# Fill tokens, x blocks and routing counts of a mixture-of-experts block with linear attention, on one Trainium2 core

## The chip, the core and the metric

The kernel runs on one core of a Trainium2 chip. A core has five engines that run their own instruction streams: TensorE (PE, matrix products, with a weight load PEld ahead of each), VectorE (DVE), ScalarE (ACT), GpSimd (POOL) and SyncE (SP, which here only issues transfers). They wait for one another by semaphores. Sixteen DMA engines move data between the chip's memory and the core's on-chip memories. The time is the device time of one execution in microseconds; lower is better.

## The reference

Input x is (8, 1024, 256) in float32: 8 sequences of 1024 tokens. It is normalised per token to xn = (x - mean) / sqrt(var + 1e-5). The output is x + attention(xn) + experts(xn).

```python
# attention: 16 heads of 16; no softmax, causal by a running sum
q = elu(xn @ Wq.T) + 1;  k = elu(xn @ Wk.T) + 1;  v = xn @ Wv.T
out   = einsum('blhd,blhde->blhe', q, cumsum(k (x) v, axis=tokens))
denom = clip(einsum('blhd,blhd->blh', q, cumsum(k, axis=tokens)), 1e-6)
attention = (out / denom) @ Wo.T

# experts: 8 of 256 -> 512 -> 256, the two with the largest logits per token
logits = xn @ Wr + br
weights, experts = top_k(logits, 2);  weights = softmax(weights)
experts(xn) = sum over the 2: weight * ((silu(xn @ W1[e]) * (xn @ W3[e])) @ W2[e])
```

## The kernel before

**Blocks and tiles.** The 8192 tokens are 16 blocks of 512 (`NBLK`), each of 4 chunks of 128. Attention runs over blocks, in 11 steps each (`block_steps`, 176 steps). The experts run over tiles of 128 tokens that go to one expert: 8192 tokens with 2 experts each make 128 full tiles, and up to 7 more because each expert's list ends in a part-filled tile, 135 in all (`NF`), of which 132 (`NM`) are always run. The first 25 tiles (`N1`) hold tokens of blocks 0 to 3 only, and so can start before the other blocks are read. The other tiles are listed once all blocks are routed.

**Start.** An order written by hand (`manual_schedule`) normalises blocks 0 to 3, turns them (features onto partitions), computes their logits, routes them (`route(0, FB)`), and lists the first 25 tiles (`first_batch`).

**The main loop**, `for j in range(NM + 1)`, then runs one expert tile per turn (`ffn_step`): it requests the tile after next's W1 and W3 (512 KB each) on SP's queue and gathers x rows and table entries on GpSimd's queue three tiles ahead; `ffn_hidden` makes gate and up products (32 matmuls, `gu_ps`), `ffn_turn` turns the next tile, and `ffn_out` multiplies the previous tile's hidden values by W2 (8 matmul passes, `y_ps`) and scales by the routing weight. `ffn_store` adds the tile's rows to the output by a GpSimd scatter with accumulation. Between the tiles attention goes on: `attend_upto(n)` runs attention up to step n. Its last phase, from `READ` = tile 22 on, spreads the rest by a quotient of the tile's number.

**Blocks 4 to 15** are handled in turns j = 0 to 11: `moments(t, 2)` computes mean and variance for two blocks at once on VectorE (`bn_stats`, then a Newton iteration for 1/sqrt in small operations), `normalise(t)` writes xn on ScalarE from the block's x into a tile of its own (two buffers), `turn(t)` transposes it on TensorE into `xnT`, which is stored to memory for attention, and `logits_of(t)` follows. `load_x(t + 3)` requests the x block three further on ScalarE's queue; x has three buffers. After every fourth block `route` takes the four: the two largest logits (a dozen VectorE operations on 128x128), counts per expert by three matmul passes into `cnt_ps`, places within an expert's list (`slot`), and the routing weights (`tab`). `route` is a generator: each `yield` is a point at which the caller can go on with other work. In the main loop it is run to its end at once.

**Fill tokens.** A part-filled tile has rows without a token. Each such row still scatters (a zero contribution), to some row of the output. Two rows of one tile must not add to the same output row, so each row p of an expert's short tile needs a token that this expert has not got. `other_tokens` finds 128 of these for each expert among the first 256 tokens: it ranks the tokens that the expert lacks (`others`, `rank_ps`), builds 16 one-hot matrices on VectorE (`at`) and multiplies each by a column of token numbers (`num_ps`). It runs at tile 8 (`LISTS - 4`). `second_batch`, from tile 12 (`LISTS`) to 21, lists the other tiles by one-hot products (`held_ps`) in parts, one part per turn, and places the fill tokens in the list's empty entries (`fill`, `fills`).

**Order.** Outside the hand-written start, a planner orders each engine's instructions by its own estimates of durations and by the order in the program; `in_order` keeps an instruction at its place. Buffers come from pools (`f_x`, `f_two`, `ps_y`) whose rotation adds waits.

Of the kernel before, what the change touches and what calls it, by code (L numbers as in the profile page):

```python
# [46 lines left out]
F32 = mybir.dt.float32  # L47
I32 = mybir.dt.int32
AF = mybir.ActivationFunctionType
ALU = mybir.AluOpType  # L50
AX = mybir.AxisListType

P = 128
# [9 lines left out]
def tile_attention_moe(  # L63
# [14 lines left out]
    nc = tc.nc  # L78
# [37 lines left out]
    f_one = ctx.enter_context(tc.tile_pool(name="f_one", bufs=1))  # L116
    f_two = ctx.enter_context(tc.tile_pool(name="f_two", bufs=2))
    f_three = ctx.enter_context(tc.tile_pool(name="f_three", bufs=3))
    f_x = ctx.enter_context(tc.tile_pool(name="f_x", bufs=3))

    early = ctx.enter_context(ExitStack())
    e_one = early.enter_context(tc.tile_pool(name="e_one", bufs=1))
# [20 lines left out]
    def load_x(t, queue):  # L143
        xbs[t] = f_x.tile([P, NCH, H], F32, tag="xb", name=f"xb{t}")
        in_order(queue.dma_start(out=xbs[t], in_=xf[t]))
# [45 lines left out]
    def iota(name, n, step, base, mult):  # L191
# [19 lines left out]
        number1, pattern=[[1, 2 * FT]], base=1, channel_multiplier=2 * FT,  # L211
        allow_small_or_imprecise_dtypes=True,
    )
    token = const.tile([P, 2], F32, name="token")
    nc.gpsimd.iota(
        token, pattern=[[P, 2]], base=1, channel_multiplier=1,
        allow_small_or_imprecise_dtypes=True,
    )
    count = f_one.tile([P, E, 1], F32, name="count")
    nc.gpsimd.iota(  # L220
        count[:, :, 0], pattern=[[N, E]], base=0, channel_multiplier=0,
# [70 lines left out]
    def normalise(t):  # L292
        xb = xbs.pop(t)
        less, rstd = (tab[:, t * NCH : (t + 1) * NCH, w] for w in (1, 2))
        xn = f_two.tile([P, NCH, H], F32, tag="xn", name="xn")
        for c in range(NCH):
            if t < FB and (c % 2 == 0 or t == FB - 1):
                nc.vector.tensor_scalar(
                    xn[:, c, :], xb[:, c, :], rstd[:, c : c + 1], less[:, c : c + 1],
                    ALU.mult, ALU.add,  # L300
                )
            else:
                nc.scalar.activation(
                    xn[:, c, :], xb[:, c, :], AF.Identity, bias=less[:, c : c + 1],
                    scale=rstd[:, c : c + 1],
                )
        scaled[t] = xn

    def turn(t):
        xn = scaled.pop(t)  # L310
# [53 lines left out]
    nc.gpsimd.memset(new, 1.0)  # L364
    nc.gpsimd.memset(new[:, :, 0:1], 0.0)
    slot = f_one.tile([P, 2, NT], F32, name="slot")
    others = f_one.tile([P, 2, E], F32, name="others")

    def route(a, b):

# [35 lines left out]
        both = f_two.tile([P, E, n], F32, tag="both", name="both")  # L406
        by_tile = both.rearrange("p e t -> p t e")
        nc.vector.tensor_tensor(by_tile, hits[:, 0], hits[:, 1], ALU.add)

        reset = new[:, :, 0:n]  # L410
        if n < MOST:
# [6 lines left out]
        )  # L418
        cnt_ps = ps_y.tile([P, E * n + E], F32, tag="y", name="cnt_ps")
        for m, what in ((upto_neg, both), (ones, run)):  # L420
            nc.tensor.matmul(
                cnt_ps[:, 0 : E * n], lhsT=m, rhs=what.rearrange("p e t -> p (e t)"),
                start=(m is upto_neg), stop=(m is ones),
            )
        nc.tensor.matmul(
            cnt_ps[:, E * n :], lhsT=ones, rhs=run[:, :, n - 1], start=True, stop=True
        )
        if a == 0:
            nc.vector.tensor_scalar(others, by_tile[:, 0:2, :], -1.0, 1.0, ALU.mult, ALU.add)
        yield  # L430
        pos = f_one.tile([P, E, n], F32, tag="pos", name="pos")
        nc.vector.tensor_tensor(
# [17 lines left out]
        nc.vector.tensor_copy(tab[:, tiles, 0], wt)  # L450
        nc.vector.tensor_tensor(tab[:, second, 0], diff, wt, ALU.mult)
        nc.vector.tensor_copy(tab[:, second, 1:3], tab[:, tiles, 1:3])
        for t in range(a, b):
            del turned[t]
        yield

    def other_tokens():


        rank_ps = ps_y.tile([P, 2, E], F32, tag="y", name="rank_ps")  # L460
        nc.tensor.matmul(
            rank_ps.rearrange("p t e -> p (t e)"), lhsT=before,
            rhs=others.rearrange("p t e -> p (t e)"), start=True, stop=False,
            skip_group_check=True,
        )
        nc.tensor.matmul(
            rank_ps[:, 1, :], lhsT=ones, rhs=others[:, 0, :], start=False, stop=True,
            skip_group_check=True,
        )
        rank = f_one.tile([P, 2, E], F32, name="rank")  # L470
        nc.vector.tensor_copy(rank, rank_ps)
        other = f_one.tile([P, E], F32, name="other")
        num_ps = ps_y.tile([P, E], F32, tag="y", name="num_ps")
        for e in range(E):
            for T in range(2):
                at = f_two.tile([P, P], F32, tag="lgT", name="at")
                nc.vector.tensor_scalar(
                    at, cols[:, 0:P], rank[:, T, e : e + 1], others[:, T, e : e + 1],
                    ALU.is_equal, ALU.mult,
                )  # L480
                nc.tensor.matmul(
                    num_ps[:, e : e + 1], lhsT=at, rhs=token[:, T : T + 1],
                    start=(T == 0), stop=(T == 1),
                )
        nc.vector.tensor_copy(other, num_ps)
        return other

    def sizes(up):

# [103 lines left out]
    def first_batch():  # L593
# [32 lines left out]
        batches[0] = tab_d[0], te_i, num_i, src_i, acc_d, src_i  # L626
        firsts.append(taken)
        yield
    def second_batch(taken, other):

        rows = sizes(True)
        left = f_one.tile([P, E], F32, name="left")
# [13 lines left out]

        short = f_one.tile([P, E], F32, name="short")
        nc.vector.tensor_scalar(short, rows, 1.5, None, ALU.is_lt)
        fill = f_one.tile([P, E], F32, name="fill")
        nc.vector.tensor_scalar(fill, other, -1.0, row[:, 0:1], ALU.add, ALU.subtract)  # L650
        nc.vector.tensor_tensor(fill, fill, short, ALU.mult)
        nc.vector.tensor_scalar(fill, fill, row[:, 0:1], None, ALU.add)
        fills = f_one.tile([P, N2], F32, name="fills")
        for e in range(E):
            mine = fills if e == 0 else f_two.tile([P, N2], F32, tag="mine", name="mine")
            nc.vector.tensor_scalar(
                mine, te, float(e), fill[:, e : e + 1], ALU.is_equal, ALU.mult
            )
            if e > 0:
                nc.vector.tensor_tensor(fills, fills, mine, ALU.add)  # L660
        num_i = const.tile([P, N2], I32, name="of2_i")
        all_held = f_one.tile([P, N2], F32, name="all_held")
        yield
        for j in range(2):
            for a in range(0, NT, 16):
                ps = ps_y.tile([P, N2], F32, tag="y", name="held_ps")
                for b in range(a, a + 16, PART):
                    at, held = one_hot(in_row, place, of_tiles, number, j, b, N2)
                    for i in range(PART):
                        nc.tensor.matmul(  # L670
                            ps, lhsT=at[:, i, :], rhs=held[:, i, :],
                            start=(b + i == a), stop=(b + i == a + 15),
                        )
                if j == 0 and a == 0:
                    nc.vector.tensor_copy(all_held, ps)
                else:
                    nc.vector.tensor_tensor(all_held, ps, all_held, ALU.add)
                yield
        nc.vector.tensor_copy(num_i, all_held)
        _, src_i = tokens(all_held, N2, NT, "2_i")  # L680
# [256 lines left out]
    with tc.manual_schedule(engines={EN.DVE, EN.Activation, EN.PE, EN.Pool}):  # L937
# [21 lines left out]
            next(q)  # L959
        routing = route(0, FB)  # L960
        next(routing)
        for o in range(KC):
            next(qs[o])
        next(ks[0])
# [173 lines left out]
    for j in range(NM + 1):  # L1138
        if j + 1 < NM:
            ffn_norm(j + 1)  # L1140
        t = FB + j
        if t < NBLK:
            if j % 2 == 0:
                with tc.issue_after(last_token[0].ins):
                    for _ in moments(t, 2):
                        pass
            normalise(t)
            if t + 3 < NBLK:
                load_x(t + 3, nc.scalar)
            turn(t)  # L1150
            logits_of(t)
            if (j + 1) % ROUND == 0:
                for _ in route(t + 1 - ROUND, t + 1):
                    pass
        if j == LISTS - 4:
            with tc.issue_after(last_token[0].ins):
                other = other_tokens()
        if j == LISTS:
            in_order(
                nc.sync.dma_start(  # L1160
                    out=tab_d[1][1 : 1 + NS * P, :].rearrange("(p i) w -> p (i w)", p=P),
                    in_=tab.rearrange("p i w -> p (i w)"),
                )
            )
            in_order(nc.sync.dma_start(out=tab_d[1][0:1, :], in_=before[0:1, 0:3]))
            lists = second_batch(taken, other)
        if LISTS <= j < READ:
            next(lists)
        if LISTS <= j < LISTS + NBLK - FB:
            t = FB + j - LISTS  # L1170
            rows = slice(t * TB, (t + 1) * TB)
            in_order(nc.sync.dma_start(out=out_rows[rows, :], in_=x_rows[rows, :]))
        if j < LISTS:
            attend_upto(3 + j // 2)
        elif j < READ:
            attend_upto(AHEAD - 2 * (READ - j - 1))
        else:
            attend_upto(AHEAD + (NBLK * STEPS - AHEAD) * (j - READ + 1) // (NM - READ - 1))
        if j == N1 + 1:
            copied.append(j)  # L1180
            in_order(nc.sync.dma_start(out=out_rows[0 : FT * P, :], in_=acc_d[:, :]))
        ffn_step(j, LATE if N1 < j <= N1 + LATE else 0)
# [53 lines left out]
```

## Time and profile before

| | us |
|---|---|
| median of the runs | 1401.64 |
| lowest and highest of 3 | 1396.12, 1402.63 |
| profiled execution, its own time | 1416.01 |
| profiled execution, span of the trace | 1414.3 |
| TensorE busy within the span | 1347.8 |
| VectorE, ScalarE, GpSimd busy | 733.5, 492.4, 517.5 |
| mean granted TensorE clock | 0.979 of full |

The profile is of one execution, here one that took longer than the timed runs. A row of its tables names a line of the kernel, an engine, and the tiles written and read; "busy" is the sum over a row's instructions, and "idle before" is how long the engine stood before them and for whom. TensorE's ends are modelled, and its clock can be granted at half: then the same matmuls show as more busy time. Busy shares are averages over stages with different limits, so a stage table (busy time in each stretch of the span) is read beside them.

### The profile page before, as it was taken

How to read it: one execution, taken by the hardware profiler on the slowest of the kernel's cores; microseconds unless marked ns; L12 is line 12 of the kernel's file. 1: busy time of each engine (PE TensorE's matmuls, PEld its weight loads, DVE VectorE, ACT ScalarE, POOL GpSimd, SP SyncE). 2: the span in 40 equal slices, each digit the busy share in tenths (PEclk: the TensorE clock that was granted, in tenths of full speed). 3: DMA queues.
4: the chain of work that ended last, by engine and by line, in shares of the span. 5: the costliest groups of instructions: out<-in, count | busy, mean ns of one | idle time of the engine just before them, and what ended most of it. 6: DMA issues, size and time to landing. Idle time of an engine off the chain costs nothing.

```text
span 1414.3 us, 27960 instructions
## 1 busy us (share of the span) xinstructions
PE 1347.8 (95%) x10932; PEld 1145.2 (81%) x10932; DVE 733.5 (52%) x1448; ACT 492.4 (35%) x914; POOL 517.5 (37%) x448
## 2 busy tenths in 40 slices
PE   6798999999999999999999999999999999999995
PEld 4667778788888888888888888888888888878885
DVE  6695468867354453536363635435353635445451
ACT  4455333132251515251523324142413325151511
POOL 2323224222434434333433343353434443343422
PEclk9999799999999999999999999999999999999998
DMA  9677455345675656565655555575655656565652
GB/s 347 191 235 223 137 161 139 105 120 160 158 220 151 175 131 149 162 164 137 159 161 135 161 149 143 129 182 144 149 162 141 157 150 157 141 173 131 150 143 42
DMA packets 129412, 223.56 MB, mean 158 GB/s; under 512 B 14818, under 2 KB 53346, under 8 KB 128994
## 3 DMA queue, kind: packets, MB, share of 16 engines
q1 hardware_dynamic: 84306, 165.95, 37.3%
q0 software_dynamic: 38064, 43.22, 19.3%
q10 hardware_dynamic: 6912, 12.58, 2.5%
q8 instruction: 90, 1.47, 0.4%
q14 instruction: 40, 0.33, 0.1%
HBM read 187.91 MB, written 44.29 MB: 164 GB/s over the span
## 4 chain that ended last, share of the span: by engine, by line
PE 82%; DVE 11%; DMA 3%; ACT 3%; issue 1%; POOL 0%; POOLq 0%; DVEq 0%; ACTq 0%
PE gu_ps L1075 32%; PE y_ps L1092 14%; PE s_ps L823 5%; PE a_ps L886 4%; PE o_ps L864 4%; PE zq L726 4%; PE zkk L741 3%; PE zkv L741 3%; DMA xb<-in_x_dram 2%; PE kv_ps L838 2%; PE held_ps L670 2%; DVE rden L802 2%; PE xg_t L1045 2%; PE o_ps L857 2%; DVE ksum L791 2%; PE den L801 2%
## 5 line engine op out<-in xcount | busy, mean ns | idle before, releaser
L1075 PEld LDWEIGHTS gu_ps<-xgT,w 128*128 128x128 f32 x4224 | 499.6, 195 | 32.0 <-issue 18.7
L1075 PE MATMUL gu_ps<-xgT,w 128*128 128x128 f32 x4224 | 518.1, 280 | 4.2 <-DVE s_sb L830 3.8
L1024 POOL DMA_INDIRECT xg<-in_x_dram,src_i x132 | 129.7, 982 | 508.7 <-ACT xgT L1047 431.6
L1092 PE MATMUL y_ps<-w_sb,hT 128*128 x1056 | 258.5, 386 | 1.3 <-DVE hT L1084 0.7
L1101 POOL DMA_INDIRECT out_dram<-y,dst_i x107 | 174.8, 1634 | 187.2 <-DVE y L1097 87.4
L1084 DVE TENSOR_TENSOR hT<-gu_ps,hT 128x512 f32<-128x512 f32 x132 | 90.4, 685 | 243.1 <-PE gu_ps L1075 226.4
L1092 PEld LDWEIGHTS y_ps<-w_sb,hT 128*128 128x128 f32 x1056 | 192.3, 193 | 25.5 <-issue 3.9
L1081 ACT ACTIVATE hT<-gu_ps 128x512 f32<-128x512 f32 x132 | 78.8, 597 | 380.8 <-PE gu_ps L1075 375.5
L830 DVE TENSOR_TENSOR s_sb<-s_ps,causal 128x512 f32<-128x512 f32 x256 | 163.2, 683 | 74.3 <-PE s_ps L823 73.3
L1097 DVE TENSOR_SCALAR y<-y_ps,entry 128x256 f32<-128x256 f32 x132 | 63.6, 482 | 135.3 <-PE y_ps L1092 135.2
L1029 POOL DMA_INDIRECT entry<-tab_d,of_i x107 | 108.0, 1009 | 32.6 <-issue 31.4
L802 DVE RECIPROCAL rden<-den 128x512 f32<-128x512 f32 x32 | 105.4, 3329 | 3.3 <-PE den L801 3.2
L823 PE MATMUL s_ps<-qm,kT 32*128 32x256 f32 x1024 | 102.7, 409 | 2.9 <-DVE rden L802 1.5
L1047 ACT COPY xgT<-xg_t 128x256 f32<-128x256 f32 x132 | 49.1, 372 | 147.9 <-PE xg_t L1045 146.3
L891 ACT COPY at<-a_ps 128x256 f32<-128x256 f32 x64 | 23.8, 372 | 193.6 <-PE a_ps L886 193.6
L823 PEld LDWEIGHTS s_ps<-qm,kT 32*128 32x128 f32 x1024 | 58.4, 184 | 36.6 <-issue 19.5
L1036 ACT ACTIVATE xg<-xg,entry 128x256 f32<-128x256 f32 x132 | 79.5, 603 | 12.0 <-DVE st L267 11.8
L886 PE MATMUL a_ps<-wo_sb,oT 128*128 128x256 f32 x256 | 68.9, 392 | 4.4 <-DVE oT L872 4.2
L1101 POOL DMA_INDIRECT acc_d<-y,src_i x25 | 42.2, 1688 | 82.2 <-DVE y L1097 46.9
L864 PE MATMUL o_ps<-s_sb,va 128*32 128x128 f32 x2048 | 70.2, 276 | 0.0
L886 PEld LDWEIGHTS a_ps<-wo_sb,oT 128*128 128x128 f32 x256 | 47.9, 193 | 14.1 <-DVE oT L872 7.4
L864 PEld LDWEIGHTS o_ps<-s_sb,va 128*32 128x32 f32 x2048 | 52.2, 109 | 8.0
(187 smaller groups left out, 1480.6 us busy)
## 6 DMA issues: line engine op xcount, KB each, us to landing
w<-in_w_dram SPq DMA_DIRECT2D x264, 512.0 KB, 4.4
xnT_d<-xnT ACTq DMA_DIRECT2D x15, 512.0 KB
xnT<-xnT_d SPq DMA_DIRECT2D x15, 512.0 KB, 5.1
out_dram<-in_x_dram SPq DMA_DIRECT2D x12, 512.0 KB
out_dram<-at POOLq DMA_DIRECT2D x12, 512.0 KB
xb<-in_x_dram ACTq DMA_DIRECT2D x9, 512.0 KB, 6.9
w_sb<-in_w_dram SPq DMA_DIRECT2D x4, 1024.0 KB
xb<-in_x_dram SPq DMA_DIRECT2D x7, 512.0 KB, 14.6
```

The costliest lines, as they stand in the source:

```text
L741: nc.tensor.matmul(z[:, i, :], lhsT=xnTs[t][:, k, bass.ts(c + i, P)], rhs=wkv_sb[:, k, a, :], start=(k == 0), stop=(k == KC - 1),)
L802: nc.vector.reciprocal(rden[:, o, :], den)
L823: nc.tensor.matmul(s_ps[r][:, hh].rearrange("p a l -> p (a l)"), lhsT=kT[rows, hh, span], rhs=qm[rows, hh, :, span], start=True, stop=True,)
L830: nc.vector.tensor_tensor(sm, s_ps[r].rearrange("p k a l -> p (k a) l"), causal_b, ALU.mult)
L864: nc.tensor.matmul(o_ps[32 * r : 32 * r + 32, hh, :], lhsT=va[:, c, 4 * hh + r, a, :], rhs=s_sb[r][:, 2 * hh + a, :], start=(first and a = ...
L886: nc.tensor.matmul(a_ps, lhsT=oT[:, hh, :], rhs=wo_sb[:, hh, :], start=(hh == 0), stop=(hh == 1),)
L1024: nc.gpsimd.indirect_dma_start(out=xg[j], out_offset=None, in_=x_rows[:, :], in_offset=bass.IndirectOffsetOnAxis(ap=src_i[:, i : i + 1], a ...
L1029: nc.gpsimd.indirect_dma_start(out=entry[j], out_offset=None, in_=table[:, :], in_offset=bass.IndirectOffsetOnAxis(ap=num_i[:, i : i + 1], ...
L1075: nc.tensor.matmul(ps[:, i, :], lhsT=w13[:, k, bass.ts(i, P)], rhs=xgT[j][:, k, :], start=(k == 0), stop=(k == KC - 1),)
L1084: nc.vector.tensor_tensor(hT, gu[1], hT, ALU.mult)
L1092: nc.tensor.matmul(y_ps, lhsT=hT[:, i, :], rhs=w2_sb[:, bass.ds(e * (IC * H) + i * H, H)], start=(i == 0), stop=(i == IC - 1),)
L1101: nc.gpsimd.indirect_dma_start(out=rows[:, :], out_offset=bass.IndirectOffsetOnAxis(ap=dst_i[:, i : i + 1], axis=0), in_=ys.pop(j), in_off ...
```

## The change

Five things are changed.

1. *Fill tokens by partition.* Instead of 128 tokens by rank, each partition p looks for one tile number T such that token T*128 + p has not been given to the expert. In `route`, `without` is 0 for tokens that the expert has and 64 - T for the others; a maximum over the tiles, kept over the rounds in `free`, gives the lowest free T per partition and expert (0 where there is none). A partition without any takes the token of partition 0, which a matmul with `ones` spreads (`at_0_ps`). `other_tokens(short)` now runs within `second_batch`, in its second part; the 3 rank passes, the 16 one-hot matrices and the 16 products are gone.
2. *x is normalised in place*, in the tile that it was read into; the two `xn` buffers go, and x has five buffers.
3. *x is read five blocks ahead*: blocks 7 and 8 are requested at the first turn, and block t + 5 after `turn(t)`.
4. *Counts a tile later.* `route` has one more `yield`, after `both`; the main loop runs it up to there after a fourth block, and the rest (counts, places, weights, `without`) at the beginning of the next turn. The counts' matmuls of these rounds keep their place in the program's order.
5. *Attention's last phase* divides by `NM - READ - 4` instead of `NM - READ - 1`.

```diff
-    f_x = ctx.enter_context(tc.tile_pool(name="f_x", bufs=3))
+    f_x = ctx.enter_context(tc.tile_pool(name="f_x", bufs=5))
...
+    from_end = iota("from_end", NT, 1, -NT, 0)
...
     def normalise(t):
-        xn = f_two.tile([P, NCH, H], F32, tag="xn", name="xn")
...
-                    xn[:, c, :], xb[:, c, :], AF.Identity, bias=less[:, c : c + 1],
+                    xb[:, c, :], xb[:, c, :], AF.Identity, bias=less[:, c : c + 1],
                     scale=rstd[:, c : c + 1],
...
     def route(a, b):
...
         nc.vector.tensor_tensor(by_tile, hits[:, 0], hits[:, 1], ALU.add)
+        yield
...
-            nc.tensor.matmul(
+            counted = nc.tensor.matmul(
...
+            if a > 0:
+                in_order(counted)
...
-        if a == 0:
-            nc.vector.tensor_scalar(others, by_tile[:, 0:2, :], -1.0, 1.0, ALU.mult, ALU.add)
...
+        without = f_one.tile([P, E, n], F32, tag="pos", name="without")
+        nc.vector.scalar_tensor_tensor(
+            without, both, -1.0, from_end[:, tiles].unsqueeze(1).to_broadcast([P, E, n]),
+            ALU.add, ALU.mult,
+        )
+        if a == 0:
+            nc.vector.tensor_reduce(free, without, op=ALU.max, axis=AX.X)
+        else:
+            most = work("most", E)
+            nc.vector.tensor_reduce(most, without, op=ALU.max, axis=AX.X)
+            nc.vector.tensor_tensor(free, free, most, ALU.max)
...
-        for e in range(E):
-            for T in range(2):
-                at = f_two.tile([P, P], F32, tag="lgT", name="at")
-                nc.vector.tensor_scalar(
-                    at, cols[:, 0:P], rank[:, T, e : e + 1], others[:, T, e : e + 1],
-                    ALU.is_equal, ALU.mult,
-                )
-                nc.tensor.matmul(
-                    num_ps[:, e : e + 1], lhsT=at, rhs=token[:, T : T + 1],
-                    start=(T == 0), stop=(T == 1),
-                )
...
+    def other_tokens(short):
+        at_0 = f_one.tile([P, E], F32, name="at_0")
+        nc.vector.tensor_scalar(at_0, free, ident[:, 0:1], None, ALU.mult)
+        at_0_ps = ps_y.tile([P, E], F32, tag="y", name="at_0_ps")
+        in_order(nc.tensor.matmul(at_0_ps, lhsT=ones, rhs=at_0, start=True, stop=True))
+        none = f_one.tile([P, E], F32, name="none")
+        nc.vector.tensor_scalar(none, free, 0.5, None, ALU.is_lt)
...
     def second_batch(taken):
...
+                if j == 0 and a == 16:
+                    fill = other_tokens(short)
+                    fills = f_one.tile([P, N2], F32, name="fills")
...
         t = FB + j
+        if t > FB and t <= NBLK and j % ROUND == 0:
+            for _ in routing:
+                pass
         if t < NBLK:
...
+            if j == 0:
+                for i in range(3, 5):
+                    load_x(t + i, nc.scalar)
             normalise(t)
-            if t + 3 < NBLK:
-                load_x(t + 3, nc.scalar)
             turn(t)
+            if t + 5 < NBLK:
+                load_x(t + 5, nc.scalar)
             logits_of(t)
             if (j + 1) % ROUND == 0:
-                for _ in route(t + 1 - ROUND, t + 1):
-                    pass
-        if j == LISTS - 4:
-            with tc.issue_after(last_token[0].ins):
-                other = other_tokens()
+                routing = route(t + 1 - ROUND, t + 1)
+                next(routing)
...
-            attend_upto(AHEAD + (NBLK * STEPS - AHEAD) * (j - READ + 1) // (NM - READ - 1))
+            attend_upto(AHEAD + (NBLK * STEPS - AHEAD) * (j - READ + 1) // (NM - READ - 4))
```

## The prediction

> **What bounds the kernel now.** I read the page's totals and its 40 slices first, then the stage table in steps of 5 us, TensorE's waits, and last the timeline where a stage looked bad.
>
> ```profile
> span 1414.3 us, 27960 instructions
> PE 1347.8 (95%) x10932; PEld 1145.2 (81%) x10932; DVE 733.5 (52%) x1448; ACT 492.4 (35%) x914; POOL 517.5 (37%) x448
> PE   6798999999999999999999999999999999999995
> PEclk9999799999999999999999999999999999999998
> ```
>
> TensorE is the bound: it stands for only 66.5 us (1414.3 - 1347.8), most of it in the first 75 us and the last 14.5. But the fifth digit of PEclk is a 7. A TensorE at half clock does half the work in the same busy time, so time can also be won where PE reads 9.
>
> ```profile
> 120.00:125.00 5.00, 1.43 (x22) 1.16 (x14) 2.54 (x6) 0.00 (x0) 0.33 (x1) 1.00 0.84 239
> 125.00:130.00 5.00, 5.00 (x30) 4.95 (x29) 4.93 (x23) 1.02 (x3) 0.00 (x0) 0.66 0.33 107
> ...
> 145.00:150.00 5.00, 3.30 (x23) 2.75 (x22) 3.89 (x19) 2.39 (x4) 3.01 (x3) 0.90 0.72 221
> 150.00:155.00 5.00, 5.00 (x20) 4.64 (x21) 2.40 (x8) 1.85 (x4) 0.53 (x1) 0.50 0.17 36
> 155.00:160.00 5.00, 5.00 (x20) 4.46 (x20) 2.34 (x10) 0.28 (x1) 0.80 (x1) 0.50 0.02 5
> ...
> 195.00:200.00 5.00, 5.00 (x15) 4.10 (x15) 2.48 (x13) 0.00 (x0) 0.43 (x1) 0.50 0.48 145
> ```
>
> Columns: the stretch, its length, busy us (and instructions) of PE, PEld, DVE, ACT, POOL, then granted clock, DMA share, GB/s. In 150 to 160 PE is busy 5.00 of 5 and does 20 matmuls where undisturbed stages do 40 to 60: half speed.
>
> ```profile
> PE gu_ps L1075 <- DVE s_sb L830: 3.6, 1, 3.6
> PE cnt_ps L421 <- DVE den L446: 1.7, 2, 1.6
> PE num_ps L481 <- DVE at L477: 1.3, 1, 1.3
> ```
>
> These rows (us in all, times, longest) hold the three longest single waits after 100 us. They stand just ahead of the three slow-clock stretches (123.9, 193.6, 148.5 us), and the change touches all three.
>
> ```profile
> 122.46 0.75 DVE L267 BATCH_NORM_STATS2 st<-xb 128x6 f32<-128x256 f32 x2 [6.10 <-DMA xb<-in_x_dram]
> 123.86 5.47 PE L1075 MATMUL gu_ps<-xgT,w 128*128 128x128 f32 x32 [3.57 <-DVE s_sb L830]
> ```
>
> VectorE stood 6.1 us at the statistics of an x block that had been requested only at 115.5; the score evictions were queued behind it, and TensorE behind those.
>
> **The change, part by part** (against the profiled execution: span 1414.3, time 1416.0; the runs' median is 1401.64, 14.4 lower, and I carry the difference in us over to it).
>
> *Fill tokens.* Out go 3 rank passes and 16 one-column products (32 L481 records, with 32 weight loads), 16 VectorE `at` builds at 0.36 us, and their ping-pong over two buffers.
>
> ```profile
> 147.20:170.20 23.00, 21.73 (x101) 19.02 (x100) 9.59 (x44) 6.23 (x13) 5.32 (x5) 0.55 0.30 78
> 147.20:170.20 23.00, 7.06 (x32) 8.91 (x32) 0.17 (x1) 0.55 0.30 78
> ```
>
> The second line is the same stretch for num_ps alone. What else it held, at the pace of clean stretches of the chain: 30 gu (32 in 3.57) 3.35; 8 y 1.73; 8 tp 0.87; 16 lg_ps 0.58; 4 a_ps 0.86; lg_t and xg_t 0.37: 7.8 us. So up to 15.2 of 23 us go: the products' issue time at half clock 6.8 (32 at 0.214), the wait 1.3, and 7.1 of slowed other work. The Trainium skill's page "TensorE: Matmul & The Clock Gate", section "What's actually happening", has the clock fall after an idle window of about 3.4 us and recover after one busy window. By it the 1.3 us gap should not slow the clock for 20 us, the slow stretch would not be the products' doing, and only 6.8 + 1.3 = 8.1 would be won. The trace differs: 0.50 for four slices of PE 5.00, lifting when the products end (1.00 from 170). I side with the trace and take 14, leaving 1.2 for what is late next: the stretch's 1.8 MB would now pass in 8 us, 230 GB/s, where 303 GB/s was seen at 140 to 145.
> Added on VectorE, in each of four routings: one 128x128 scalar_tensor_tensor (0.29, as L397) and a reduce (0.28, as L391), a max of 8 in three (0.15): 2.7 us in all; at the lists nine 128x8 operations at 0.16, 1.5 us, and one matmul pair. In the first routing they stand ahead of the list of first tiles, where VectorE is busy 4.5 of 5: +0.4 (0.57 less the 0.17 of `others`). At 200 to 235 VectorE is busy 4.5 to 5.0 of 5: its extra (0.7 + 1.5, less 0.4 of old fill steps) can reach TensorE; bounds 0 and 2, I take 1. The longer iota on GpSimd lies in the first 5 us, before it waits for VectorE: 0.
>
> *x in place, five ahead.* Blocks 7 and 8 are now requested together behind the second tile's xg scaling (53.6 us) instead of at 58.2 and 66.3; later ones once the transposes of the block five earlier are done. The ACT queue issues them (0.39 us each) behind the same copies that wait for those transposes anyway. In-place writing takes nothing from ACT: the same 128x256 operations. But the order of VectorE moves too: each block's statistics stand one block earlier. Laid over the old trace, requests come at about 54, 55, 61, 70, 81, 89, 98, 109, 117 us for blocks 7 to 15; with 7.2 us to landing (median of this transfer), block 12 lands at 96 and VectorE gets there at 94; block 13 at 105 against 102; 14 at 116 against 113; 15 at 124, now behind the score evictions. So the waits do not vanish: about 2 to 4 us each, where before they were 1.2, 3.0, 6.1 and 1.8. The 3.6 us stall and the 1.7 us of clock after it (0.34 of 5 us) go, 5.3; new stalls around 95 to 103 give back some 3 (evictions are behind block 12's statistics). Bounds: -5.3 and +2; I take -2.5.
> Early on, the x statistics of block 8 stand ahead of the Newton steps for blocks 6 and 7, and ACT's first operation on block 6 now stands ahead of block 5's xnT copies. With block 8 landed at 63, the steps end at 68.5 and those copies start at 69.1; TensorE came to them at 68.56, so +1. Bounds -1 and +4 (each us that block 8 is later is a us here).
>
> *Routing counts a tile later.* The counts' matmuls (before: waits of 1.6 at 193 and about 0.9 at 100, then the clock at 0.84 and 0.50 over 190 to 200, 3.3 us) now follow the next tile's work. In the last round only 3 score passes (0.4 us) and tile work stand between, and VectorE's chain of twelve steps is 3.9 us long, so about 0.8 of wait stays. SP's table transfer and the output copies wait a little longer for `tab`, with up to two tiles of weights already issued. Of 1.6 + 3.3 + 0.9 I take 3.5; bounds 1 and 5.8.
>
> *Attention ends sooner.* The quotient reaches all steps at tile 127 instead of 130 (three tiles by the formula). The tail:
>
> ```profile
> 1392.28 1.80 POOL L894 DMA_DIRECT2D out_dram<-at  x2 [5.04 <-ACT xgT L1047]
> 1397.29 1.59 POOL L1101 DMA_INDIRECT out_dram<-y,dst_i  x1 [3.21 <-DVE hT L1084]
> 1402.45 1.55 POOL L1101 DMA_INDIRECT out_dram<-y,dst_i  x1 [3.56 <-DMA out_dram<-y,dst_i]
> 1407.07 1.55 POOL L1101 DMA_INDIRECT out_dram<-y,dst_i  x1 [3.07 <-DMA out_dram<-y,dst_i]
> ```
>
> Each store waits for the one before it (steps of 5.2 and 4.6). The pair of attention adds delays the y of 1393.3 to 1397.3, and the last y, ready at 1400.3, goes out 6.7 later. With the pair six stores from the end, a tile without attention is 3.57 + 0.22 + 1.73 = 5.5 us, a store 4.9: the 4.0 of arrears shrinks by 0.6 a tile to 1.8, and the last y leaves 1.8 + 4.9 - 1.7 = 5.0 after it is ready. Gain 1.7, I take 2; bounds 0 and 4.
>
> **Sum:** -14 + 0.4 + 1 - 2.5 + 1 - 3.5 - 2 = -19.6, say -20: 1416 to 1396 for the profiled execution, 1401.6 to 1381.6 for the runs. Half a per cent, about what a measurement of this kernel can tell from no change, is 7 us: faster is below 1394.6, slower above 1408.6.
>
> **Rivals.**
> *The slow clock is not the products' doing* (the page's rule). Then 8 goes instead of 14, and the clock shares after the other waits stay too: about -11, 1391. For it: clocks of 0.50 and 0.66 at 800 and 880 with no products near. Against: it began and ended with them. 0.20.
> *The x waits stay whole*: VectorE's new order uses up the distance, B turns to +2: -15, 1386. 0.13.
> *Slower: the stall moves and takes the clock with it.* The statistics of blocks 12, 13 and 14 stand ahead of score evictions. If each holds TensorE over 1.3 us and each such gap costs the clock for 20 us, as the one at 147 did (10 us), that is 3 x 12.5 = 37 against the 19 won by the products, counts and tail: 1420. It decides where a block lands over 3.5 us after VectorE is there. Against: gaps of 1.2 to 1.7 us at 63, 560 and 1180 us left the clock at 1.00. 0.04.
> *Most of the gain is eaten by the planner's new order* in the 1000 us where TensorE is full (15 us of small waits there, any of which may grow): within 0.5%. 0.03.
> The forecast itself: 0.60, with its own range 1372 to 1391.
>
> **Numbers.** Low end: products 15.2, reads 5.3, counts 5.8, tail 4, early 0: -30 and a few us of the random clock drops at 800 to 890 (5 us): 1368. High end: products 8.1, counts 1, reads +2, early +4, lists +2, tail 0: -1; two in ten may lie outside, so 1394. Faster 0.87, same 0.09, slower 0.04: the rivals at 1391 and 1386 have tails into "same", the fourth is there, and the third alone is slower.
>
> **What would show it.** Right: no L481 rows; clock 1.00 over what was 147 to 170 and that work done in 8 to 9 us; the s_sb wait of 3.6 gone, DVE's waits for xb still some 8 to 12 us in sum; cnt_ps waits under 1; six y stores after the last attention add, the last leaving about 5 us after its y. Wrong: a clock of 0.50 for 10 us or more between 90 and 170 without the products, or a TensorE wait above 2 us on s_sb near 95 to 105.

## The result, and the profile after

The changed kernel takes 1395.05 us (median of 22 runs, 1389.26 to 1401.49), the kernel before beside it 1402.76 (22 runs): a ratio of 0.9943, 95% interval 0.9926 to 0.9961, about 8 us or half of a per cent. The forecast was 20 us. The kernel before takes 1403 to 1412 us in the sets of runs below, so ratios to the kernel before of the same set are compared, or runs of one set. A ratio can differ from the quotient of two medians, by up to 0.3%; where that matters, both are given.

The two profiled executions lie 18.1 us apart (1416.01 and 1397.95), close to the forecast, and that is the trap of this case: part of it is a clock loss that most executions do not seem to have, and part is luck, for two terms were wrong in opposite directions. The totals of the page after:

```profile
span 1396.2 us, 27887 instructions
PE 1333.8 (96%) x10898; PEld 1134.8 (81%) x10898; DVE 732.0 (52%) x1446; ACT 489.2 (35%) x912; POOL 522.2 (37%) x448
PE   6699999999999999999999999999999999999996
PEclk9899999999999999999999999999999999999998
```

The 7 in the fifth slice of PEclk is gone. In the 5 us table (stretch, length, busy us and instructions of PE, PEld, DVE, ACT, POOL, clock, DMA share, GB/s) the stretch where the products stood reads:

```profile
100.00:105.00 5.00, 3.39 (x35) 2.70 (x35) 3.33 (x17) 1.25 (x3) 0.00 (x0) 1.00 0.53 144
...
145.00:150.00 5.00, 5.00 (x46) 4.78 (x39) 0.88 (x2) 1.73 (x4) 1.66 (x3) 1.00 0.86 223
150.00:155.00 5.00, 5.00 (x52) 3.40 (x50) 2.12 (x5) 1.34 (x3) 3.11 (x3) 1.00 0.84 264
155.00:160.00 5.00, 5.00 (x68) 4.68 (x68) 2.22 (x5) 0.60 (x1) 0.00 (x0) 1.00 0.27 35
```

Full speed and 46 to 68 matmuls a row, where there were 20. TensorE's waits between 75 and 235 us (total, times, longest):

```profile
PE cnt_ps L419 <- DVE both L405: 1.3, 2, 0.9
PE cnt_ps L419 <- DVE run L413: 1.2, 1, 1.2
PE gu_ps L1075 <- DVE s_sb L829: 1.1, 2, 0.6
...
PE cnt_ps L419 <- DVE den L444: 0.4, 1, 0.4
```

The 3.6 us wait for the score evictions is gone. The counts still wait, 2.9 us in all. VectorE's waits for x blocks in the same part of the run:

```profile
101.93 0.43 DVE L264 BATCH_NORM_STATS2 st<-xb 128x6 f32<-128x256 f32 x1 [1.54 <-DMA xb<-in_x_dram]
115.15 0.75 DVE L264 BATCH_NORM_STATS2 st<-xb 128x6 f32<-128x256 f32 x2 [1.16 <-DMA xb<-in_x_dram]
121.89 0.75 DVE L264 BATCH_NORM_STATS2 st<-xb 128x6 f32<-128x256 f32 x2 [0.92 <-DMA xb<-in_x_dram]
```

3.6 us where it was 12.1. To add it up I cut both traces at the starts of the y scalings (L1097), one for each expert tile; "y 15" is the start of number 15, counted from 0. Half of each half-clock stretch in the trace is counted as clock loss and taken out. Before to after: clock losses up to y 15 went from 20.5 to 5.1 us, the rest up to y 15 from 253.0 to 244.2. From y 15 to the last y the changed kernel is slower: 1121.3 to 1126.6 with the clock taken out, and 1.7 more of clock; the tail behind the last y went from 14.4 to 13.5. Together -15.4 - 8.8 + 5.3 + 1.7 - 1.0 = -18.2. Where TensorE's idle time is taken out too, what is left is called its work. Two things are to be explained: is a clock loss of 20.5 usual, and what costs 5.3 where the prediction expected a gain.

### The profile page after: what moved, and what is told of

Same layout as the page of the kernel before. It is cut to its first block, busy times and chain, and to the rows that moved or that the text cites. A ratio compares the mean times of both kernels' runs of the same rounds, so it can differ in the third digit from the quotient of the medians.

```text
span 1396.2 us, 27887 instructions
## 1 busy us (share of the span) xinstructions
PE 1333.8 (96%) x10898; PEld 1134.8 (81%) x10898; DVE 732.0 (52%) x1446; ACT 489.2 (35%) x912; POOL 522.2 (37%) x448
## 5 line engine op out<-in xcount | busy, mean ns | idle before, releaser
L1075 PE MATMUL gu_ps<-xgT,w 128*128 128x128 f32 x4224 | 512.3, 279 | 1.5 <-DVE s_sb L829 1.1
L1024 POOL DMA_INDIRECT xg<-in_x_dram,src_i x132 | 132.6, 1005 | 540.5 <-ACT xgT L1047 440.5
L1092 PE MATMUL y_ps<-w_sb,hT 128*128 x1056 | 251.6, 380 | 0.9 <-DVE hT L1084 0.4
L1097 DVE TENSOR_SCALAR y<-y_ps,entry 128x256 f32<-128x256 f32 x132 | 63.7, 482 | 135.1 <-PE y_ps L1092 134.8
L822 PE MATMUL s_ps<-qm,kT 32*128 32x256 f32 x1024 | 107.7, 412 | 3.4 <-DVE rden L801 2.0
L822 PEld LDWEIGHTS s_ps<-qm,kT 32*128 32x128 f32 x1024 | 61.7, 185 | 39.0 <-issue 19.5
```

Of the source, the lines that this page charges most:

```text
L822: nc.tensor.matmul(s_ps[r][:, hh].rearrange("p a l -> p (a l)"), lhsT=kT[rows, hh, span], rhs=qm[rows, hh, :, span], start=True, stop=True,)
L1024: nc.gpsimd.indirect_dma_start(out=xg[j], out_offset=None, in_=x_rows[:, :], in_offset=bass.IndirectOffsetOnAxis(ap=src_i[:, i : i + 1], a ...
L1075: nc.tensor.matmul(ps[:, i, :], lhsT=w13[:, k, bass.ts(i, P)], rhs=xgT[j][:, k, :], start=(k == 0), stop=(k == KC - 1),)
L1092: nc.tensor.matmul(y_ps, lhsT=hT[:, i, :], rhs=w2_sb[:, bass.ds(e * (IC * H) + i * H, H)], start=(i == 0), stop=(i == IC - 1),)
```

## Experiments

**Is the profiled execution typical?** The kernel before was run again unchanged (e1), and with the fill change alone (e2: of the diff above only `from_end`, `free`, `without`, `other_tokens(short)` and its call in `second_batch`).

> The kernel before, unchanged, profiled and timed once more. Theory A (the one profiled execution of before was untypical: its half clock over 147 to 170 and 193 to 200 us was bad luck, and the change loses what the prediction took from it): the mean granted clock of its other executions lies near 0.987, against 0.979 in the first profile, its time near 1402, and the new profile has no half-clock stretch over 10 us between 140 and 210. Theory B (the one-column products bring the half clock every time, and some other part of the change gives the gain back): the clock is near 0.979 in most executions, and the new profile shows 0.50 over num_ps again.

> The kernel before with the new fill tokens alone (reads, counts and pace as before). A: the products' work at full clock is 4.3 us by the two traces (y store 0 to 27: 356.9 against 352.6 us of undisturbed work) and the wait ahead of them 1.3, less about 1 for the added VectorE work: some 5 us below before, 1397. B: 14 below before, 1388.

e1: ratio 0.9995 (0.9971 to 1.002). The mean clock of its 22 executions was 0.9847, the median time 1408.26; but the profile again came out at 1416.62, clock 0.979, with a half clock of 20.5 us over the products. Each execution's granted clock was measured, and in this set 19 of 73 executions of the kernel before had 0.982 or less, with a median of 1418.2, against 1407.0 for the others. Over all sets of the experiments, on two chips, it was 40 of 142. (The expectations of e8 and e13 below say 17 of 73 and 30 of 131; counted so it is 19 and 35.) The border is set by eye: the clocks run from 0.973 to 0.993 without a gap. A half clock of 20.5 us costs 10.2 us, or 0.007 of the mean clock, which is what parts the profile's 0.979 from the usual 0.986 to 0.988. So the half clock over the products is real and comes back, as B says, but by these clocks the usual execution does not have it, as A says. No profile of such an execution of the kernel before was taken, so this is not shown directly. e2: 0.9963 (0.9942 to 0.9985), 5.2 us, as A expected (its median is 3.5 us below e1's); 1 of its 22 executions was at 0.982 or less. Between y 4 and y 9 its trace has 3.5 us less than e1's beside the clock (52.2 against 55.7).

e13 is a third profile of the kernel before:

> The kernel before, profiled a third time. 30 of 131 executions so far were at a clock of 0.982 or less, and both profiles are of these. If the half clock over the products is a matter of chance: three in four that this profile has none over 5 us between 140 and 210, with the 32 product records at about 0.11 us apart instead of 0.21, and a span near 1402. If the profile itself brings it: the half clock is there a third time.

1412.57 us, clock 0.982, and the half clock a third time, for 23.9 us. Three profiles of three against 40 executions of 142 would be a chance of 2 in 100; whether being profiled favours it stays open.

**Are the products to blame?** e8 gives each product 64 equal columns in place of one; the planner places a few neighbours otherwise.

```diff
-num_ps = ps_y.tile([P, E], F32, tag="y", name="num_ps")
+num_ps = ps_y.tile([P, E, 64], F32, tag="y", name="num_ps")
...
-num_ps[:, e : e + 1], lhsT=at, rhs=token[:, T : T + 1],
+num_ps[:, e, :], lhsT=at, rhs=token[:, T : T + 1].to_broadcast([P, 64]),
...
-nc.vector.tensor_copy(other, num_ps)
+nc.vector.tensor_copy(other, num_ps[:, :, 0])
```

> The kernel before with 64 equal columns instead of one behind each of its 16 products (only the first is read), so that TensorE works longer behind each weight load. 17 of 73 executions of the kernel before were at a clock of 0.982 or less, about 11 us above the rest, and both profiles of it have the half clock over the products. If the products' idle columns hold the clock at a half: none or almost none of these executions is at 0.982 or less, and the profile has no half-clock stretch over 7 us between 140 and 210; the other executions cost up to 1.8 us more (32 records at half of a 128-column pass of 0.112). If the 1.3 us gap ahead of them or chance does: about one in four stays.

0.998 (0.9958 to 1.0001), and none of 20 executions was at 0.982 or less, where the kernel before had 5 of 27 on the same chip. (Of 142 executions of the kernels of this document that have no such products, 2 were.) Rows of e13 (the kernel before), then of e8:

```profile
145.00:150.00 5.00, 2.44 (x14) 1.98 (x14) 3.87 (x19) 1.79 (x4) 2.75 (x3) 0.86 0.78 190
150.00:155.00 5.00, 5.00 (x21) 4.55 (x20) 1.91 (x7) 1.85 (x4) 0.79 (x1) 0.50 0.12 27
155.00:160.00 5.00, 5.00 (x20) 4.46 (x20) 2.59 (x10) 0.00 (x0) 0.13 (x1) 0.50 0.02 5
```

```profile
145.00:150.00 5.00, 2.66 (x21) 2.24 (x21) 4.10 (x21) 2.00 (x4) 2.76 (x3) 1.00 0.78 218
150.00:155.00 5.00, 4.93 (x35) 4.33 (x35) 4.21 (x19) 1.85 (x4) 0.78 (x1) 1.00 0.12 27
155.00:160.00 5.00, 5.00 (x49) 4.13 (x48) 2.48 (x13) 2.27 (x5) 2.60 (x2) 1.00 0.52 135
```

and e8's product records and the wait ahead of them:

```profile
L481 PE MATMUL num_ps<-token,at x32: 219/275/323, 148.8 to 158.1; 128*128 128x64 f32 x32
```

```profile
PE num_ps L481 <- DVE at L477: 1.3, 1, 1.3
```

The same gap of 1.3 us stands ahead of the products, in a row as idle as that of the kernel before (2.66 of 5), and the clock stays at 1.00. So neither the gap nor the products' presence is enough: what e8 takes away is the single column behind each weight load, and with it the half clock goes, in one profile against three that have it and in the clocks of its executions. Why it comes in about one execution of four only is not known.

**Where does the end lose?** e3 and e6 are the changed kernel with the old quotient:

```diff
-attend_upto(AHEAD + (NBLK * STEPS - AHEAD) * (j - READ + 1) // (NM - READ - 4))
+attend_upto(AHEAD + (NBLK * STEPS - AHEAD) * (j - READ + 1) // (NM - READ - 1))
```

> The changed kernel with attention's last steps spread to the end again (NM - READ - 1). Prediction: 2 us slower than after (the last y leaves 6.7 instead of 5.0 us after it is ready), 1397. Rival from the traces (after needs 4.0 us more of undisturbed TensorE work and 1.3 more of waits for the same instructions behind y 27, mostly at s_ps, and ends only 0.8 sooner behind its last y): 3 to 4 us faster than after, 1391.

> The changed kernel, unchanged, beside the kernel before on the chip of these runs, where the kernel before takes 1408 instead of 1403. Theory A (the change is worth what its parts show: fill 3.4, reads some 10, pace -1, counts 1) : a ratio of 0.990, 1394. Rival (the change is worth 8 us on any chip, as first measured): 0.9943, 1400.

> The changed kernel with attention's last steps spread to the end again, timed beside the changed kernel. From the traces (behind y 27, granted clock taken out: 982.4 against 984.3 us, and a tail behind the last y of 14.4 against 13.6): 1 us faster than the changed kernel. Prediction: 2 us slower.

e3: 0.9894 (0.9842 to 0.9947). On another chip e5, the changed kernel: 1394.4, 0.991 (0.988 to 0.9939); e6: 1388.84, 0.9881 (0.9848 to 0.9913). The old pace is about 5 us faster, not 2 slower (e5 to e6: 5.6 by the medians, and 1126.7 to 1121.4 in the traces from y 15 on with the clock taken out). Why, is seen in one tile of the changed kernel with two score passes (a pass is the 16 `s_ps` matmul records of one chunk of tokens), TensorE's timeline:

```profile
1107.72 1.08 PE L863 MATMUL o_ps<-s_sb,va 128*32 128x128 f32 x32
1108.73 0.71 PE L822 MATMUL s_ps<-qm,kT 32*128 32x256 f32 x6
1110.38 1.13 PE L885 MATMUL a_ps<-wo_sb,oT 128*128 128x256 f32 x4 [0.94 <-DVE oT L871]
1111.44 1.13 PE L822 MATMUL s_ps<-qm,kT 32*128 32x256 f32 x10
```

and VectorE's:

```profile
1106.72 1.89 DVE L829 TENSOR_TENSOR s_sb<-s_ps,causal 128x512 f32<-128x512 f32 x3 [0.57 <-PE s_ps L822]
1108.53 0.41 DVE L842 TENSOR_TENSOR kv<-kv_ps,heads 128x256 f32<-128x256 f32 x1
1108.98 0.43 DVE L844 TENSOR_TENSOR kv<-kv 128x256 f32<-128x256 f32 x1
1109.32 0.68 DVE L829 TENSOR_TENSOR s_sb<-s_ps,causal 128x512 f32<-128x512 f32 x1
1109.92 0.41 DVE L871 SCALAR_TENSOR_TENSOR oT<-rden,o_ps 128x256 f32<-128x256 f32 x1
```

The second pass starts as the products that use the first end (1108.73), stops after six of its 16 records, and goes on at 1111.44, 2 us later, with only `a_ps` between: VectorE is busy without a gap with the first pass's evictions (0.63 us each), `kv` and `oT`, and with both passes in one tile no gate, up or y matmuls stand between them to cover it. A block's steps have score passes at 5, 6, 8 and 9, so a tile with both 5 and 6, or both 8 and 9, holds two; it is called a double tile here. By the formula attention's last phase has 4 double tiles at the old pace and 8 at the changed one. Three more paces follow from that: the same line with `NM - READ - 2` (e9), with `NM - READ - 3` (e10), and with -4 and this (e11), where n is the quotient:

```diff
+if n % STEPS in (6, 9) and steps_made[0] < n - 1:
+    n -= 1
```

> The changed kernel with NM - READ - 2 in attention's last pace, so that its last step falls in tile 129 instead of 127. By the formula a block's 11 steps have score passes at 5, 6, 8 and 9; a tile that holds two of them (5 with 6, or 8 with 9) occurs 4 times with -1, 8 times with -4, 11 times with -3 and never with -2. Theory P (such a tile costs TensorE about 1.3 us, as 5.1 us for 4 of them between -1 and -4 behind y 15): no tile with 28 or more score matmuls, behind y 15 some 10 us less than the changed kernel's 1126.6 (granted clock taken out), and about 10 us faster than it, a ratio to before near 0.986. Rival (an earlier end costs by itself, 1.6 us for each tile): between the old pace and the changed one, 3 us faster than the changed kernel.

> The changed kernel with NM - READ - 3: 11 tiles with two score passes, against 8 in the changed kernel. Theory P: 4 us slower than the changed kernel, a ratio to before near 0.996. Rival (an earlier end costs by itself): 1.6 us faster than the changed kernel.

> The changed kernel with its own pace (last step in tile 127), except that a second score pass of one tile waits for the next tile: 0 such tiles. Theory P: as fast as NM - READ - 2 or up to 1 us faster, for the tail of the earlier end; a ratio near 0.986. Rival: as the changed kernel, 0.993.

> The changed kernel once more, as the measure of the three paces on one chip. From two earlier chips: a ratio to before of 0.991 to 0.994.

| pace | last step in tile | double tiles of the last phase | work from y 15 to the last y, us | ratio to before (95%) |
|---|---|---|---|---|
| -1 (e3, e6) | 130 | 4 | 1105.4, 1104.3 | 0.9894, 0.9881 |
| -2 (e9) | 129 | 0 | 1102.1 | 0.9849 (0.9819 to 0.9879) |
| -3 (e10) | 128 | 11 | 1111.7 | 0.9968 (0.9944 to 0.9993) |
| -4 (first profile, e5, e12) | 127 | 8 | 1107.7, 1107.9, 1109.8 | 0.9943, 0.991, 0.9938 |
| -4, apart (e11) | 127 | 0 | 1102.9 | 0.9878 (0.9848 to 0.9909) |

Score matmuls from 250 us to the end (busy us of PE, PEld, DVE) of e11 and e12, which end attention in the same tile, then of e9 (no double tile) and e10 (11):

```profile
250.00:1380.00 1130.00, 83.78 (x928) 49.50 (x928) 148.00 (x233) 1.00 0.59 151
```

```profile
250.00:1390.00 1140.00, 92.80 (x928) 53.92 (x928) 147.79 (x232) 1.00 0.59 150
```

```profile
250.00:1390.00 1140.00, 79.30 (x928) 46.91 (x928) 148.06 (x232) 1.00 0.59 150
250.00:1400.00 1150.00, 99.48 (x928) 57.24 (x928) 147.73 (x232) 0.99 0.58 149
```

and what score weight loads waited for evictions (us, times) in e11 and then e10:

```profile
  PEld s_ps L822: 0.9, 3
```

```profile
  PEld s_ps L822: 4.8, 17
```

The same 928 records take 9.0 us longer with double tiles, and the same early end is 9 us faster without them (1395.13 against 1404.12). The rival, that an early end costs by itself, falls. In TensorE's work a double tile costs 0.6 to 0.9 us (the three profiles of the changed kernel against e11: 4.8, 5.0 and 6.9 us for 8 tiles). By time it is 1.1 (9 us for 8), near the 1.3 that was expected. What makes the rest is not shown: idle time is 21.9 us in e12 against 18.7 in e11, but the two other profiles of the changed kernel have 18.8 too. Nor is all of the work above that of double tiles: e9 and e11, both without any, differ by 0.8 us of work and 4.5 of score matmuls, and by 3.8 in their medians. What -2 wins over -1 is not settled: the intervals overlap, and the traces, those of e14 to e16 below included, show 2 to 4 us less work against 1 to 5 more of idle.

**What are the reads worth?** e4 restores xn in its own buffer and reads three ahead, in the changed kernel:

```diff
-f_x = ctx.enter_context(tc.tile_pool(name="f_x", bufs=5))
+f_x = ctx.enter_context(tc.tile_pool(name="f_x", bufs=3))
...
+xn = f_two.tile([P, NCH, H], F32, tag="xn", name="xn")
...
+if t + 3 < NBLK:
+    load_x(t + 3, nc.scalar)
 turn(t)
-if t + 5 < NBLK:
-    load_x(t + 5, nc.scalar)
```

> The changed kernel with x normalised into its own buffer and read three blocks ahead. Prediction: +1.5 (2.5 of waits come back, 1 of the early stage goes): 1396.5. Rival (five ahead fetches early what the narrow start cannot use; TensorE's 10.5 us wait at 50 and the 5.6 at 63 stay in both, and the waits of before for x blocks at 113 and 122 return): +4 to +5, 1399.5. If the clock falls with the 3.6 us gap at 124, a half-clock stretch of 3.4 to 20 us follows it.

1.001 (0.9976 to 1.0045) against 0.991 to 0.994 of the changed kernel: without this part nothing is left of the gain. e14 makes the same edit at the pace -2; e15, at that pace too, keeps the five buffers and the writing in place and makes only the last part of it, the `load_x` lines (in all three edits the two early requests of the first turn go too); e16 is their measure.

> The kernel of e9 (NM - READ - 2) with x normalised into its own buffer and read three blocks ahead. Prediction: 1.5 us slower than e9's kernel. Rival, from the traces of e4 and e3 (to y 15, granted clock taken out, 251.4 against 243.7 us, and 3.4 more of clock): 8 to 11 slower.

> The kernel of e9 with x normalised in place but read three blocks ahead, as before. If the distance of the reads is what wins: as slow as e14. If the order that in-place writing brings wins (no second buffer to wait for): as fast as e16. The distance is likelier: 8 slower than e16.

> The kernel of e9 once more, as the measure of e14 and e15 on their chip: a ratio to before of 0.982 to 0.988.

Medians 1390.67, 1388.39 and 1383.0; ratios 0.9886, 0.9875 and 0.9839, each known to 0.4%. The slowest execution of e16 (1386.57) is below the fastest of e14 (1388.35); e15 (1384.61 to 1393.75) overlaps both, so its place rests on the traces. VectorE's waits for x blocks between 85 and 170 us, in e14, e15, e16:

```profile
DVE st L264 <- DMA xb<-in_x_dram: 10.6, 3, 5.0
```

```profile
DVE st L264 <- DMA xb<-in_x_dram: 8.6, 3, 3.7
```

```profile
DVE st L264 <- DMA xb<-in_x_dram: 2.5, 3, 1.2
```

Up to y 15 they need 246.9, 244.7 and 242.3 us beside clock losses of 6.8, 6.8 and 3.4. So the reads' part is worth about 8 us, of which the distance has the larger half or more. From y 0 to y 15 alone, clock included, it is 174.4, 173.8 and 169.1, so 5.3, of which the distance has 4.7; ahead of y 0 two profiles of one kernel can differ by more than the rest (84.4 us to y 0 in e9, 76.7 in e16).

**The counts at once** (e7: no `yield` behind `both` and no `in_order` for the counts either):

```diff
-for _ in routing:
-    pass
...
-routing = route(t + 1 - ROUND, t + 1)
-next(routing)
+for _ in route(t + 1 - ROUND, t + 1):
+    pass
```

> The changed kernel with each routing run to its end in the tile where it begins, as before. Prediction: 3.5 us slower than the changed kernel, with TensorE waits for the counts of about 1.6 and 0.9 again. Rival (the clock losses of 3.3 that the prediction put on these waits were the random ones; only the waits are won, and some of them stay): 1 us slower or less.

0.9925 (0.9892 to 0.9959) against e5's 0.991 on that chip: not told apart by time. From y 0 to y 15 the traces show 171.7 us against 169.7, and 1.7 of these 2.0 are a half clock behind this wait of e7:

```profile
PE cnt_ps L418 <- DVE den L441: 1.6, 1, 1.6
```

## Why the prediction failed

The mechanisms were mostly right; the sum failed in its first and last terms and in how it was carried over, and its term for the reads was too small. That the profiled pair came out near the forecast is luck in part: the reads gave more than foreseen and the pace took what they gave.

- **"I carry the difference in us over"**, from one profiled execution to the median, is the step that failed first. The profile was of the slower quarter of the executions, 14.4 us above the median, and its excess is about the clock loss that the change takes away (15.4 up to y 15). That could not be won in executions that, by their clocks, did not have it.
- **Fill tokens, -14** (-12.6 with the +0.4 and +1 of the added operations, which e2 holds too). Measured -5.2 by the ratio, -3.5 by the medians (e2). In the profiled pair between y 4 and y 9 clock losses alone went from 11.9 us to none. The products' issue at half clock (6.8) comes to 3.4 of TensorE's work with the clock taken out (50.5 to 47.1 between y 4 and y 9, e1 to e2); the 7.1 of slowed other work is there in about one execution of four, judged by the clocks. Siding with the trace was right for the cause, and wrong for the size. Two readings were slightly off: the rank products are two, not three (the pages count 34 matmul records less), and the 1.3 us ahead of the products is not among the three longest waits after 100 us, for `den` waits 1.5 at 562 us, at full clock. The rule of the Trainium skill's page "TensorE: Matmul & The Clock Gate" ("What's actually happening"), by which, as the prediction read it, the products were not to blame, would have given 8.1: nearer for the median, but for a wrong reason, as e8 shows. The same section calls the window free-running; whether a phase against it decides which executions fall was not tried.
- **Lists, +1.** From y 12 to y 15: 48.8 to 50.0 us at full clock. Right. The +0.4 at the start lies within what the first y varies between profiles of one kernel (76.9, 79.4 and 83.0 us in the three of the changed one).
- **Reads, -2.5 and +1.** Requests came as worked out (54.4, 54.9, 63.6, 71.5, 79.9, 87.5, 95.9, 108.9, 116.4 us), and new waits at blocks 13, 14 and 15; the one foreseen at block 12 did not come. But they were 0.9 to 1.5 us where 2 to 4 were expected, and reached TensorE as 1.2 at the counts (the scan stands behind the wait at 101.93). The wait of 0.6 for score evictions, at 97.1, is ahead of all three. So the 3 us of give-back was mis-sized. Without it the prediction's 5.3 stands, which is also the size that e14 and e16 show from y 0 to y 15. The early +1 is not seen. Worth about 8 in all; the part ahead of y 0 is not explained.
- **Counts, -3.5.** About 2 by one pair of traces, not resolved by time. The waits, said to fall under 1, are 2.9 in all against 2.6 before; what is won is mostly the clock behind the long one.
- **Tail, -2.** Here the sign was wrong: +5. The stores follow as forecast, six behind the last attention add:

```profile
1356.40 1.85 POOL L893 DMA_DIRECT2D out_dram<-at  x2 [2.72 <-ACT hT L1081]
...
1384.50 1.55 POOL L1101 DMA_INDIRECT out_dram<-y,dst_i  x1 [3.81 <-DVEq L1193]
1389.06 1.55 POOL L1101 DMA_INDIRECT out_dram<-y,dst_i  x1 [3.01 <-DMA out_dram<-y,dst_i]
```

The last y was ready at 1383.2 and left 5.9 us later, for 6.7 before and 5.0 foreseen. But the prediction followed the divisor to its end only. It also sets which steps share a tile in the 100 tiles ahead, and doubled the tiles with two score passes from 4 to 8. The prediction's fourth rival named small waits under TensorE's full stretch as what could eat the gain, without this mechanism.

Sum by the runs: -5 (fill) - 8 (reads) - 2 (counts) + 5 (pace) = -10, against 8 to 13 less by the ratios of the three sets and about 8 by their medians. With -2 in place of -4 the change gives 0.9849 and 0.9839, 20 to 23 us, faster than both kernels.

## What to carry to other kernels

Before a profile's clock losses are put into a sum, compare that execution's time and mean clock with the other runs: a profile 1% above the median, as here, can show the very stretch that the median lacks. A pace written as a quotient is a pattern, not only an end: count which steps it puts together over the whole run, and try its neighbours, for one more or less can turn 0 collisions into 11. Evictions that TensorE waits for, such as those of two score passes in a row, want other matmuls between.

## What was not expected of the hardware

- Apart from the idle tail, half-clock stretches came in multiples of 3.4 us in every trace (3.4, 6.8, 10.2, 20.5, 23.9), those over 11 us only over the one-column products, with TensorE busy 5.00 of 5. Products of 64 columns ran at full clock, and their 32 records spanned 9.3 us (148.8 to 158.1) where one-column records at half clock spanned 18.2 (148.5 to 166.7).
- The kernel before took medians of 1405.95, 1408.07 and 1411.72 in three sets on one chip, and 1402.74 on another. In e1's profile TensorE idled 30.1 us ahead of the first y, in the first profile 24.9.
